# First image's statistics by channel and half with long rows for the matrices, and layer 1's transfers by four columns

## The chip, the cores and the metric

The kernel runs on one core of one Trainium2 chip. The metric is the device time of one execution in microseconds (us), the median over several runs. Everything is in float32.

## What is computed

The input x has 4 images of 64 channels and 256 x 256 pixels. Two layers follow each other, each with a group norm over pairs of channels in front and a residual sum behind:

```python
def _gn(v, G=32, eps=1e-5):
    g = v.reshape(B_, G, C_ // G, H_, W_)
    m = jnp.mean(g, axis=(2, 3, 4), keepdims=True)
    s = jnp.var(g, axis=(2, 3, 4), keepdims=True)
    return ((g - m) / jnp.sqrt(s + eps)).reshape(v.shape)

x = x + _L0_conv_ref(_gn(x), L0_conv_w1, L0_conv_w_dw, L0_conv_w_out, L0_conv_ln_w, L0_conv_ln_b)
x = x + _L1_conv_ref(_gn(x), L1_conv_w_ih, L1_conv_w_hh, L1_conv_b_ih, L1_conv_b_hh)
```

Layer 0 takes 64 channels to 384 by a 1x1 convolution, applies a 3x3 depthwise convolution, splits into q, k and v, multiplies the Fourier transforms of q and k in patches of 8 x 8 pixels (a circular convolution), applies a layer norm over the channels, multiplies by v and projects back to 64 channels. Layer 1 is a gated recurrent unit that runs over the columns of the image, one after the other. The state of a column's pixel is its new value; its input are the three neighbours in the column before:

```python
def step(prev_col, cur_col):
    nb = jnp.concatenate([pad, prev_col, pad], axis=1)
    x = jnp.concatenate([nb[:, :-2], nb[:, 1:-1], nb[:, 2:]], axis=-1)
    new = _gru_cell(x.reshape(B * H, 3 * Cf), cur_col.reshape(B * H, Cf), w_ih, w_hh, b_ih, b_hh).reshape(B, H, Cf)
    return (new, new)
```

## The kernel before

The host hands over x with columns ahead of rows, and besides that xh, a copy cut into windows of 10 x 10 pixels (100 values, HALO) for every 8 x 8 patch. All instructions of an engine run in the order in which the program names them (the class InOrder); a DMA is issued by an engine's queue in that same order, so a DMA that waits holds up everything that the program puts after it on that queue. The queues used are SP's (most transfers), POOL's (xq, seen, the writing of the matrices) and ACT's (weights).

**Preamble.** Three things are prepared. First, the depthwise taps and the Fourier matrices are merged into matrices of 100 x 64 per channel: 32 rounds of small matmuls into PSUM (psb), each copied by ACT into the tile ts, 96 KB per partition. Three DMAs on POOL's queue write ts to the DRAM tile t_all (3 x 3200 KB), laid out [3, 8, 100, 1024], so that one fetch of 16 channels' matrices later reads one contiguous block of 400 KB (100 rows of 4 KB). Second, the statistics of the first image: it is read in 8 steps of 2 MB (xc), each by two DMAs of 64 partitions, one for the left half of the image and one for the right (function piece, lines 206 to 210), and VectorE takes bn_stats of 512 elements. norm_of_pieces (line 84) then averages over the pairs of channels and the halves with a 128 x 128 matrix (avg2) and leaves scale and shift in sc0. Third, the weights: hh, w1, g, wo, ln and taps on ACT's queue at the start, wi, wh and bias on the same queue after the statistics, in thirteen DMAs.

**Layer 0** runs in 32 blocks (n), eight for each image. The pools for its tiles (big, xp, tp, wk) are opened after the preamble's are closed, in the same memory. A block's input xq comes in four quarters (load, line 296, on POOL's queue; normalize, line 303, on ACT or VectorE, with small memsets on POOL at the image's edges). Then:

- pointwise, 3 x 16 units: the 1x1 convolution, evicted to the tile h;
- circular, twice: transform multiplies h with matrices t, which fetch (line 329) brings four ahead from t_all on SP's queue; products q * k on VectorE in buffers of the pool wk (seven of 4 KB per partition, lines 289 and 290); inverse back to the pixels in z;
- values: v from h with the last eight matrices;
- layer_norm in slices between the other work, with its statistics in the tile lnst;
- finish(n - 1), which lies in the next block: residual loads xr (x of the block, SP's queue), gate transposes and multiplies, project adds to xr, and store writes it to the DRAM tile x1 (two DMAs of 64 partitions for each of four units u; the last unit's store is put off to the circular stage).

Beside this the next image's statistics are taken: look loads a piece of 4 columns (two DMAs of 64 partitions on POOL's queue) into a wk buffer, count takes bn_stats of it, four times per block (24 of the 32 blocks).

**Layer 1** runs over 256 columns w. x1 is [4, 64, 256, 256], columns ahead of rows. Two images stand side by side on the 128 partitions, channels of one on 0 to 63 and of the other on 64 to 127, with the pairs of images arranged differently in even and odd columns (SLOTS), so that each of TensorE's four 64 x 64 quarters has work. A pair of columns is loaded by three DMAs (load_columns, one of 128 partitions for the even column, two of 64 for the odd one), in rows of 1 KB; stored likewise by three (in add, line 767, after POOL's sum with the raw values); and two more DMAs copy the normalized columns to the other half of the partitions (xt, in normalize, line 748). Columns are loaded 16 ahead and normalized 8 ahead, in tiles of eight columns (WB). column(w) issues the matmuls of the gates r, n and z in two parts of the column; state(w, part) applies sigmoid, tanh and the update on ACT and VectorE.

Of the kernel before, what the change touches and what calls it, by code (L numbers as in the profile page):

```python
# [83 lines left out]
def norm_of_pieces(nc, st, t, psum, eps, sc):  # L84

    m_all, d, total, mean = t[:, 128:136], t[:, 136:144], t[:, 144:145], t[:, 145:146]
    nc.vector.tensor_copy(m_all, st[:, :, 0])
    nc.vector.tensor_reduce(total, m_all, mybir.AxisListType.X, ALU.add)  # L90
    yield
    pm = psum()
    nc.tensor.matmul(pm, lhsT=t[:, 0:P], rhs=total, start=True, stop=True)
    nc.vector.tensor_copy(mean, pm)
    nc.vector.tensor_tensor(d, m_all, mean.to_broadcast([P, 8]), ALU.subtract)
    nc.vector.tensor_tensor(d, d, d, ALU.mult)
    nc.vector.tensor_tensor(d, d, st[:, :, 1], ALU.add)
    nc.vector.tensor_reduce(total, d, mybir.AxisListType.X, ALU.add)
    yield
    pv = psum()  # L100
    nc.tensor.matmul(pv, lhsT=t[:, 0:P], rhs=total, start=True, stop=True)
    nc.scalar.activation(sc[:, 1:2], pv, AF.Sqrt, bias=eps, scale=1.0)
    nc.vector.reciprocal(sc[:, 1:2], sc[:, 1:2])
    nc.vector.scalar_tensor_tensor(sc[:, 0:1], mean, -1.0, sc[:, 1:2], ALU.mult, ALU.mult)
    yield
# [57 lines left out]
def tile_conv_then_gru(  # L163
# [14 lines left out]
    avg2: bass.AP,  # L178
    out: bass.AP,
# [5 lines left out]
    x1 = dram.tile([B, C, W, H], F32, tag="x1", name="x1")  # L185


    t_all = dram.tile([3, 8, HALO, 16 * NS], F32, tag="t_all", name="t_all")


    ident = const.tile([P, P], F32, tag="ident", name="ident")
    make_identity(tc.nc, ident)
    hh_sb = const.tile([P, P], F32, tag="hh", name="hh_sb")
    nc.scalar.dma_start(hh_sb, hh)
    eps = const.tile([P, 1], F32, tag="eps", name="eps")
    nc.gpsimd.memset(eps, EPS)
    w1_sb = const.tile([P, HID], F32, tag="w1", name="w1_sb")
    nc.scalar.dma_start(w1_sb, w1.rearrange("a c o -> (a c) o"))
    g_sb = const.tile([P, 2, 2, NS], F32, tag="g", name="g_sb")
    nc.scalar.dma_start(g_sb, g12.rearrange("a s r n p -> (a s) r n p"))  # L200
    wo_sb = const.tile([P, 2, C], F32, tag="wo", name="wo_sb")
    nc.scalar.dma_start(wo_sb, w_out.rearrange("a f t c -> (a f) t c"))
    ln_sb = const.tile([P, 2, 2], F32, tag="ln", name="ln_sb")
    nc.scalar.dma_start(ln_sb, ln.rearrange("a f n t -> (a f) n t"))

    def piece(of, b, i, w, n):

        for half in range(2):
            w0 = half * (W // 2) + i * (W // 16) + w
            yield slice(half * C, (half + 1) * C), of[b, :, w0 : w0 + n, :].rearrange("c w h -> c (w h)")  # L210
# [6 lines left out]
    with tc.tile_pool(name="xa", bufs=3) as xa, tc.tile_pool(name="sta", bufs=1) as sta, tc.tile_pool(  # L217
# [4 lines left out]
        for i in range(4):  # L222
            nc.scalar.dma_start(bt[32 * i : 32 * i + 9], taps[i])
            nc.sync.dma_start(wd[32 * i : 32 * i + 9], w_dw)
        avg4 = sta.tile([P, 1024], F32, tag="avg4", name="avg4_0")
        nc.sync.dma_start(avg4[:, 0:P], avg2)
        ts = sta.tile([HALO, 3 * P, NS], F32, tag="ts", name="ts")
        banks = bps.tile([P, 8, 512], F32, tag="b", name="psb")
        for i in range(32):
# [14 lines left out]
        for i in range(3):  # L244
            nc.gpsimd.dma_start(
                t_all[i].rearrange("n p k -> p n k"),
                ts[:, i * P : (i + 1) * P].rearrange("p (n c) k -> p n (c k)", n=8),
            )
        for i in range(8):
            xc = xa.tile([P, 4096], F32, tag="xc", name=f"xc_{i}")  # L250
            for at, of in piece(x, 0, i, 0, 16):
                nc.sync.dma_start(xc[at], of)
            for k in range(8):
                nc.vector.bn_stats(bn0[:, k, :], xc[:, 512 * k : 512 * k + 512])
            nc.vector.bn_aggr(st0[:, i, :], bn0)
        for _ in norm_of_pieces(nc, st0, avg4, lambda: banks[:, 0, 0:1], eps, sc0[:, 0]):
            pass
    wi = const.tile([P, 9, C], F32, tag="wi", name="wi")
    wh = const.tile([P, 3, C], F32, tag="wh", name="wh")
    for a in range(2):  # L260
        at = slice(a * C, (a + 1) * C)
        for g in range(3):
            nc.scalar.dma_start(wi[at, 3 * g : 3 * g + 3, :], w_ih[g].rearrange("t c o -> c t o"))
            nc.scalar.dma_start(wh[at, g, :], w_hh[g])
    bias_sb = const.tile([P, 6], F32, tag="bias", name="bias_sb")
    nc.scalar.dma_start(bias_sb, bias.rearrange("a o n -> (a o) n"))
# [5 lines left out]

    st1 = const.tile([P, NBLK, 2], F32, tag="st1", name="st1")
    with ExitStack() as s:
        big = s.enter_context(tc.tile_pool(name="big", bufs=1))
        xp = s.enter_context(tc.tile_pool(name="xp", bufs=4))
# [18 lines left out]
        xq = {}  # L295

        def load(n, jq):

            t = xp.tile([P, 16, HALO], F32, tag="xq", name=f"xq_{n}_{jq}")
            nc.gpsimd.dma_start(t, xh[n, :, 16 * jq : 16 * jq + 16, :])  # L300
            xq[n, jq] = t

# [26 lines left out]
        def fetch(count):  # L329
            while len(streamed) < min(count, NBLK * 24):  # L330
                m, r = divmod(len(streamed), 24)
                t = tp.tile([P, 16, NS], F32, tag="t", name=f"t_{m}_{r}")
                nc.sync.dma_start(t[0:HALO].rearrange("p c k -> p (c k)"), t_all[order[r][0], order[r][1]])
# [124 lines left out]
        def layer_norm(n):  # L458

            st = big.tile([P, 2, NP // 2, 6], F32, tag="lnst", name=f"lnst_{n}")  # L460
# [128 lines left out]
        def store(n, u, xr):  # L589
            b, r0, c0 = n // 8, (n % 8) * 32 + (u // 2) * 8, (u % 2) * P  # L590
            for g in range(2):
                nc.sync.dma_start(
                    x1[b, :, r0 + 16 * g : r0 + 16 * g + 8, c0 : c0 + P],
                    xr[g * C : (g + 1) * C],
                )

        def look(n, k, t):

            for at, of in piece(x, n // 8 + 1, n % 8, 4 * k, 4):
                nc.gpsimd.dma_start(t[at], of)  # L600

        def count(n, k, t):
            for i in range(2):
                nc.vector.bn_stats(bn0[:, 2 * k + i, :], t[:, 512 * i : 512 * i + 512])
            if k == 3:
                nc.vector.bn_aggr(st0[:, n % 8, :], bn0)
# [12 lines left out]
        for jq in range(4):  # L619
            load(0, jq)  # L620
        for jq in range(4):
            normalize(0, jq)
        norm = None
        for n in range(NBLK + 1):
# [4 lines left out]
            if n == NBLK:  # L629
                for _ in norm:  # L630
                    pass
            if n:
# [5 lines left out]
            more = n // 8 + 1 < B  # L638
            if more:
                seen = work(f"seen0_{n}")  # L640
                look(n, 0, seen)
            circular(n, 0, lambda sp: count(n, 0, seen) if more and sp == 1 else None)
            if more:
                seen = work(f"seen1_{n}")
                look(n, 1, seen)
            for unit in range(16):
                pointwise(n, 1, unit, unit in (5, 8, 11, 14))
                if more and unit in (8, 14):
                    count(n, unit // 7, seen)
                    look(n, unit // 7 + 1, seen)  # L650
# [3 lines left out]
            def beside(sp):  # L654
                next(norm)
                if more and sp == 1:
                    count(n, 3, seen)
# [3 lines left out]
            if more and n % 8 == 7:  # L661
                t = work(f"avg4_{n}")
                nc.gpsimd.dma_start(t[:, 0:P], avg2)
                image = norm_of_pieces(nc, st0, t, lambda: psum()[:, 0, 0:1], eps, sc0[:, n // 8 + 1])
# [53 lines left out]
    with ExitStack() as s:  # L718
        rawp = s.enter_context(tc.tile_pool(name="raw", bufs=3))
# [5 lines left out]
        def columns(m, w):  # L725

            yield m[:, :, w, :].rearrange("(k a) c h -> (a c) k h", k=NPAIR), slice(0, P), 0
            for half in range(2):
                b0 = SLOTS[1][0][half]
                yield m[b0 : b0 + 2, :, w + 1, :].rearrange("b c h -> c b h"), slice(half * C, half * C + C), 1  # L730

        def load_columns(w):
            n, i = w // WB, w % WB
            if i == 0:
                raws[n] = rawp.tile([P, 2, WB, H], F32, tag="raw", name=f"raw_{n}")
            for of, at, j in columns(x1, w):
                nc.sync.dma_start(raws[n][at, :, i + j], of)
# [10 lines left out]
        def normalize(w, slot):  # L748
            n, i = w // WB, w % WB
            if i == slot == 0:  # L750
                new_columns(n)
            nc.scalar.activation(
                xns[n][:, slot, i],
                raws[n][:, slot, i],
# [4 lines left out]
            if slot and i % 2:  # L759

                for half in range(2):
                    nc.sync.dma_start(
                        xts[n][half * C : (half + 1) * C, i - 1 : i + 1],
                        xns[n][(1 - half) * C : (2 - half) * C, half, i - 1 : i + 1],
                    )

        def add(w):
            n, i = w // WB, w % WB
            nc.gpsimd.tensor_tensor(
                raws[n][:, :, i], raws[n][:, :, i], stcols[n][:, :, i, 1 : H + 1], ALU.add  # L770
            )
            if i % 2:
                for of, at, j in columns(out, w - 1):
                    nc.sync.dma_start(of, raws[n][at, :, i - 1 + j])
# [152 lines left out]
```

## Time and profile before

| | us |
|---|---|
| median of 3 runs | 5883.06 |
| lowest and highest run | 5861.34, 5891.94 |
| the profiled execution | 5869.95 |
| its span in the trace | 5868.2 |
| preamble, up to the first matmul of layer 0 | 138.3 |
| layer 0, up to layer 1's first loads | 4338.1 |
| layer 1, first matmul with xt | 4357.8 |
| TensorE's granted clock, mean | 0.994 |

Of the page's six parts the first two (busy time of each engine, and the span in forty slices of 147 us) tell which engine is full in which stage. Parts 3 and 6 hold the transfers: SP's queue carried 520152 packets and 633.59 MB (40.0% of the sixteen DMA engines' time), POOL's 37776 packets and 165.24 MB (9.5%), and the instruction queue 996 packets and 16.32 MB. All compute instructions have one line number, that of the class InOrder, so groups go by the names of tiles: psring is the PSUM ring of layer 0, pshr, psni, pshz and pshn are the gates' banks in layer 1, raw and xn the columns as loaded and normalized.

### The profile page before, as it was taken

How to read it: one execution, taken by the hardware profiler on the slowest of the kernel's cores; microseconds unless marked ns; L12 is line 12 of the kernel's file. 1: busy time of each engine (PE TensorE's matmuls, PEld its weight loads, DVE VectorE, ACT ScalarE, POOL GpSimd, SP SyncE). 2: the span in 40 equal slices, each digit the busy share in tenths (PEclk: the TensorE clock that was granted, in tenths of full speed). 3: DMA queues.
4: the chain of work that ended last, by engine and by line, in shares of the span. 5: the costliest groups of instructions: out<-in, count | busy, mean ns of one | idle time of the engine just before them, and what ended most of it. 6: DMA issues, size and time to landing. Idle time of an engine off the chain costs nothing. (4 is left out here: it accounts for less than half of the span.)

```text
span 5868.2 us, 278629 instructions
## 1 busy us (share of the span) xinstructions
PE 5479.9 (93%) x127196; PEld 4762.6 (81%) x127196; DVE 4080.5 (70%) x9593; ACT 3475.4 (59%) x4604; POOL 500.8 (9%) x797
## 2 busy tenths in 40 slices
PE   2999999999999999999999999999979999999998
PEld 1878888888788878887888888878868888888888
DVE  2776777777767777777677767766667777776766
ACT  2556566665565656655655666556556666666655
POOL 0000000000000000000000000000002122222222
PEclk9999999999999999999999999999989999999999
DMA  8455555555555555555555454544444444444443
GB/s 225 135 156 147 151 151 155 154 142 152 157 147 154 150 151 159 141 150 159 150 152 150 140 143 126 142 139 125 137 114 116 116 116 117 115 117 113 116 114 81
DMA packets 561916, 818.04 MB, mean 139 GB/s; under 512 B 41353, under 2 KB 435373, under 8 KB 559677
## 3 DMA queue, kind: packets, MB, share of 16 engines
q1 hardware_dynamic: 520152, 633.59, 40.0%
q0 software_dynamic: 37776, 165.24, 9.5%
q8 instruction: 996, 16.32, 1.2%
q10 hardware_dynamic: 2808, 1.38, 0.1%
q14 instruction: 184, 1.50, 0.1%
HBM read 622.46 MB, written 144.05 MB: 131 GB/s over the span
## 5 line engine op out<-in xcount | busy, mean ns | idle before, releaser
L157 PEld LDWEIGHTS psring<-h,t 100*32 100x32 f32 x40960 | 1334.1, 115 | 294.0 <-issue 175.2
L157 PE MATMUL psring<-h,t 100*32 100x128 f32 x40960 | 1445.2, 274 | 105.9 <-issue 37.7
L157 PE MATMUL psring<-w_sb,xq 64*100 64x128 f32 x24576 | 1403.2, 271 | 55.7 <-POOL xq L157 40.2
L157 PEld LDWEIGHTS psring<-w_sb,xq 64*100 64x100 f32 x24576 | 1357.6, 164 | 117.0 <-issue 50.2
L157 ACT COPY h<-psring 100x1024 f32<-100x1024 f32 x1274 | 1205.5, 1027 | 161.4 <-PE psring L157 155.2
L157 DVE TENSOR_TENSOR pr<-psring,q 128x512 f32<-128x512 f32 (+1 forms) x576 | 463.3, 857 | 308.8 <-PE psring L157 234.8
L157 DVE BATCH_NORM_STATS2 lnst<-z 128x6 f32<-128x64 f32 x4096 | 545.4, 214 | 117.6 <-ACT z L157 117.6
L157 DVE TENSOR_TENSOR z<-z,lnm 128x1024 f32<-128x1024 f32 x512 | 612.7, 1218 | 8.8
L157 ACT COPY q<-psring 128x1024 f32<-128x1024 f32 x256 | 259.3, 1013 | 596.8 <-PE psring L157 358.9
L157 ACT ACTIVATE z<-pshz,b_rz 128x288 f32<-128x288 f32 (+7 forms) x510 | 242.6, 476 | 519.8 <-PE pshz L157 519.7
L157 PE MATMUL pshr<-st,wi 64*64 64x144 f32 (+7 forms) x12240 | 510.5, 270 | 34.9 <-issue 20.9
L157 PE MATMUL psni<-st,wi 64*64 64x144 f32 (+7 forms) x12240 | 510.4, 270 | 24.4 <-issue 22.4
L157 PE MATMUL pshz<-st,wi 64*64 64x144 f32 (+7 forms) x12240 | 510.8, 270 | 23.1 <-issue 21.9
L157 ACT COPY z<-psring 128x2048 f32<-128x2048 f32 x128 | 238.9, 1867 | 446.7 <-PE psring L157 441.7
L157 PE MATMUL psring<-pr,g_sb 32*64 32x512 f32 x8192 | 494.8, 594 | 5.7 <-issue 5.5
L157 ACT ACTIVATE y<-psring,ln_sb 128x512 f32<-128x512 f32 x512 | 372.5, 781 | 200.5 <-PE psring L157 197.0
L157 PEld LDWEIGHTS psni<-st,wi 64*64 64x64 f32 x12240 | 446.5, 133 | 45.5 <-issue 34.4
L157 PEld LDWEIGHTS pshr<-st,wi 64*64 64x64 f32 x12240 | 422.3, 133 | 52.3 <-issue 49.5
L157 DVE COPY h<-psring 100x1024 f32<-100x1024 f32 x262 | 320.3, 1223 | 198.7 <-PE psring L157 194.7
L157 PEld LDWEIGHTS pshz<-st,wi 64*64 64x64 f32 x12240 | 424.9, 133 | 37.3 <-issue 36.4
L157 DVE SCALAR_TENSOR_TENSOR g<-z,xn 128x288 f32<-128x288 f32 (+7 forms) x510 | 218.4, 428 | 311.9 <-ACT z L157 310.0
L157 POOL TENSOR_TENSOR raw<-raw,st 128x512 f32<-128x512 f32 x256 | 303.7, 1186 | 1146.0 <-ACT xn L157 548.1
(98 smaller groups left out, 7377.9 us busy)
## 6 DMA issues: line engine op xcount, KB each, us to landing
t<-t_all SPq DMA_DIRECT2D x768, 400.0 KB
xq<-in_xh POOLq DMA_DIRECT2D x128, 800.0 KB, 4.6
xr<-in_x SPq DMA_DIRECT2D x256, 256.0 KB
x<-xr SPq DMA_DIRECT2D x256, 256.0 KB
seen<-in_x POOLq DMA_DIRECT2D x192, 256.0 KB, 4.1
raw<-x SPq DMA_DIRECT2D x128, 256.0 KB
raw<-x SPq DMA_DIRECT2D x256, 128.0 KB
xt<-xn SPq DMA_DIRECT2D x256, 128.0 KB
```

The lines of the kernel that those rows point to most:

```text
L157: return self.tc.keep_in_program_order(got(*args, **kwargs))
```

## The change

**Preamble.** x is read by (channel, half of the image) on all 128 partitions, in 16 steps of 1 MB with one DMA each and five buffers. norm_of_pieces gets two matrices (sums): one averages in the order of these partitions, the other carries the mean over to the order of the normalization. The DRAM tile t_all becomes [3, 100, 8, 1024]: ts is written in rows of 32 KB, and a fetch reads 100 rows of 4 KB at a pitch of 32 KB. The first two of the three writes are named before the third kind is computed. The pool xp is opened ahead of the preamble's pools, and the first block's four loads of xq come right after the writes on POOL's queue. The weights move to SP's queue, between the sixth and seventh piece of x, in one DMA each.

**Layer 0.** store writes even and odd columns to separate halves of x1, in four DMAs per unit instead of two. Pieces of the next image are loaded on 128 partitions; those of two columns go into lnst, which becomes one tile for the whole layer, and two of four columns go into one wk buffer.

**Layer 1.** x1 and the output are [2, 4, 64, 128, 256], even and odd columns apart (the host puts them together again). Four columns are loaded by three DMAs in rows of 2 KB, stored by three, and copied to xt by two, spread over four steps of w. Tiles of raw columns hold four columns, in seven buffers. Before the first step four columns are normalized instead of nine; the function ahead then catches up to eight.

```diff
-    x1 = dram.tile([B, C, W, H], F32, tag="x1", name="x1")
-    t_all = dram.tile([3, 8, HALO, 16 * NS], F32, tag="t_all", name="t_all")
+    x1 = dram.tile([2, B, C, W // 2, H], F32, tag="x1", name="x1")
+    t_all = dram.tile([3, HALO, 8, 16 * NS], F32, tag="t_all", name="t_all")
+    layer0 = ExitStack()
+    xp = layer0.enter_context(tc.tile_pool(name="xp", bufs=4))
...
     def piece(of, b, i, w, n):
-        for half in range(2):
-            w0 = half * (W // 2) + i * (W // 16) + w
-            yield slice(half * C, (half + 1) * C), of[b, :, w0 : w0 + n, :].rearrange("c w h -> c (w h)")
+        w0 = i * (W // 16) + w
+        return of[b].rearrange("c (a w) h -> (c a) w h", a=2)[:, w0 : w0 + n, :].rearrange("p w h -> p (w h)")
...
+        def keep_matrices(i):
+            nc.gpsimd.dma_start(
+                t_all[i].rearrange("p n k -> p (n k)"),
+                ts[:, i * P : (i + 1) * P].rearrange("p c k -> p (c k)"),
+            )
...
-        for i in range(3):
-            nc.gpsimd.dma_start(
-                t_all[i].rearrange("n p k -> p n k"),
-                ts[:, i * P : (i + 1) * P].rearrange("p (n c) k -> p n (c k)", n=8),
-            )
-        for i in range(8):
-            xc = xa.tile([P, 4096], F32, tag="xc", name=f"xc_{i}")
-            for at, of in piece(x, 0, i, 0, 16):
-                nc.sync.dma_start(xc[at], of)
+            if i == 15:
+                keep_matrices(0)
+                keep_matrices(1)
+        keep_matrices(2)
+        for jq in range(4):
+            load(0, jq)
+        def seen_piece(i):
+            xc = xa.tile([P, 2048], F32, tag="xc", name=f"xc_{i}")
+            nc.sync.dma_start(xc, piece(x, 0, i // 2, i % 2 * 8, 8))
+            for k in range(4):
+                nc.vector.bn_stats(bn0[:, i % 2 * 4 + k, :], xc[:, 512 * k : 512 * k + 512])
+            if i % 2:
+                nc.vector.bn_aggr(st0[:, i // 2, :], bn0)
...
     pm = psum()
-    nc.tensor.matmul(pm, lhsT=t[:, 0:P], rhs=total, start=True, stop=True)
+    for i in range(2):
+        nc.tensor.matmul(pm[:, i : i + 1], lhsT=t[:, P * i : P * i + P], rhs=total, start=True, stop=True)
...
             for g in range(2):
-                nc.sync.dma_start(
-                    x1[b, :, r0 + 16 * g : r0 + 16 * g + 8, c0 : c0 + P],
-                    xr[g * C : (g + 1) * C],
-                )
+                at = r0 // 2 + 8 * g
+                for odd in range(2):
+                    nc.sync.dma_start(x1[odd, b, :, at : at + 4, c0 : c0 + P], xr[g * C : (g + 1) * C, odd::2])
...
+            def beside_first(sp):
+                if more and sp in (0, 3):
+                    count(n, 2 * (sp // 3), seen)
+                    look(n, 2 * (sp // 3) + 2, seen)
+
+            circular(n, 0, beside_first)
             if more:
-                seen = work(f"seen1_{n}")
-                look(n, 1, seen)
+                four = work(f"seen_{n}")
+                look(n, 8, four)
...
-            if slot and i % 2:
+            if slot and i % 4 == 3:
                 for half in range(2):
                     nc.sync.dma_start(
-                        xts[n][half * C : (half + 1) * C, i - 1 : i + 1],
-                        xns[n][(1 - half) * C : (2 - half) * C, half, i - 1 : i + 1],
+                        xts[n][half * C : (half + 1) * C, i - 3 : i + 1],
+                        xns[n][(1 - half) * C : (2 - half) * C, half, i - 3 : i + 1],
                     )
...
+        def ahead(w):
+            return min(2 * w + 4, w + WB + 1, W)
...
             add(w)
-            if i % 2 and w + 2 * WB < W:
-                load_columns(w + 2 * WB - 1)
+            if i >= 2:
+                store_columns(w - i, i - 2)
+            elif i == 0 and w:
+                store_columns(w - 4, 2)
+            if i < 3 and w - i + 2 * WB < W:
+                load_columns(w - i + 2 * WB, i)
+        store_columns(W - 4, 2)
```

## The prediction

> **What bounds the kernel now.** I read the page first (busy shares and the forty slices), then a table of busy time by stretches of the span, then the waits of TensorE in each stage, then the timeline where the stretches show TensorE idle. From the page:
>
> ```profile
> PE 5479.9 (93%) x127196; PEld 4762.6 (81%) x127196; DVE 4080.5 (70%) x9593; ACT 3475.4 (59%) x4604; POOL 500.8 (9%) x797
> ...
> PE   2999999999999999999999999999979999999998
> ...
> DMA  8455555555555555555555454544444444444443
> ```
>
> TensorE is full in every slice but two: the first (147 us, two tenths) and the one where layer 0 hands over to layer 1 (seven tenths). Of 5868.2 us it is idle 388 us. The stretches say where:
>
> ```profile
> 20.00:40.00 20.00, 15.35 (x106) 6.36 (x108) 10.43 (x18) 11.56 (x12) 0.00 (x0) 1.00 1.01 216
> ...
> 60.00:80.00 20.00, 0.00 (x0) 0.00 (x0) 10.43 (x18) 0.00 (x0) 0.00 (x0) 1.00 1.01 250
> 80.00:100.00 20.00, 1.00 (x4) 0.95 (x4) 11.59 (x25) 0.00 (x0) 0.00 (x0) 1.00 0.98 285
> 100.00:120.00 20.00, 0.14 (x1) 0.05 (x1) 0.32 (x2) 1.55 (x2) 0.00 (x0) 1.00 0.73 225
> ```
>
> (Columns: PE, PEld, DVE, ACT, POOL busy; granted clock; DMA share; GB/s.) The preamble is bound by the DMA engines: they are full, yet move only 216 GB/s while the first image is read alone. Then a second hold, after that read is over:
>
> ```profile
> 97.95 0.56 PE L157 MATMUL psb<-avg 128*128 128x1 f32 x2 [42.60 <-issue]
> ...
> 126.77 52.92 SPq L157 DMA_DIRECT2D t<-t_all  x11
> ...
> 127.57 2.17 POOL L157 DMA_DIRECT2D xq<-in_xh  x4 [70.28 <-DMA t<-t_all]
> ...
> 138.31 6.25 PE L157 MATMUL psring<-w_sb,xq 64*100 64x128 f32 x64 [38.17 <-POOL xq L157]
> ```
>
> The statistics are done at 102 us, but layer 0's first tiles of input (xq) are requested only at 127.6 us, when the matrices have landed in t_all, and the first matmul of layer 0 waits until 138.3. So 36 us lie between statistics and work.
>
> Layer 0 (180 to 4280 us) has TensorE busy 3970 of 4100 us; a block takes (4284.1 - 245.2) / 31 = 130.3 us, and all named waits of TensorE there add to 127 us, 46 of them with no releaser, 36 on ACT's last copy of h, 15 on the matrices. Nothing in it is bound by a transfer for long. Layer 1, in a part without its ends (4400 to 5700 us), first stretches and then waits:
>
> ```profile
> 4400.00:5700.00 1300.00, 1211.14 (x40650) 1153.83 (x40646) 918.50 (x2209) 792.25 (x1768) 267.04 (x277) 1.00 0.42 116
> 5700.00:5765.00 65.00, 59.25 (x1984) 56.15 (x1980) 44.39 (x108) 38.37 (x86) 13.13 (x13) 1.00 0.42 115
> 5765.00:5810.00 45.00, 42.78 (x1432) 40.29 (x1428) 32.59 (x79) 28.05 (x63) 8.57 (x9) 1.00 0.32 83
> 5810.00:5850.00 40.00, 39.66 (x1369) 38.70 (x1365) 30.40 (x74) 19.77 (x46) 9.51 (x8) 1.00 0.21 57
> ```
>
> ```profile
> PE pshz L157 <- issue: 26.0, 47, 1.2
> PE pshr L157 <- issue: 25.6, 53, 1.2
> PE psni L157 <- issue: 19.5, 27, 1.7
> PE pshr L157 <- DVE st L157: 13.4, 7, 1.9
> ```
>
> TensorE waits for no transfer here. Its gaps are "issue": 71 us in 1300, in 127 pieces, and in the timeline they stand at multiples of about 4 us. A column is 184 matmuls and as many weight loads in 5.88 us, some 63 instructions per us, so 256 of them last 4.1 us. As the loads run out (share 0.42, 0.32, 0.21) the rate rises from 31.3 to 31.8 and 34.2 matmuls per us.
>
> [...] the two half-image pieces of 2 MB come every 10.1 us, 207 GB/s, with the engines' share at 1, while the 128-partition xq loads run at 312 to 315 GB/s. [...]
>
> **The change, part by part.**
>
> *1. Preamble.* Removed: the half-partition reads, twelve weight DMAs on ACT's queue (100 to 127 us, ACT can't normalize behind them), and the wait of xq for the memory that the matrices' buffer gives back, since xq's pool is now allocated ahead of it. Added: one 128x128x1 matmul (0.3 us), nine constant loads among the image's pieces on SP. What must move before the first matmul: image 16.8 MB, matrices 9.8 (issued at 44 and 56 us as before, paced by ACT's copies), constants and taps 1.5, first xq 0.8: 28.9 MB. The rate is unknown for this mix; nearest rows: 312 to 331 GB/s (xq alone; 85 to 95 us), 250 (60 to 80 us, held by the half-partition stream). I take 300: 96 us from 2.5, then 2 us to land, 1.7 normalize, 0.4 memset: about 103 us instead of 138.3. DVE isn't the bound (16 pieces x 2.6 us = 42 us). At 330 GB/s the first matmul is at 94, at 250 at 122. If [...]the image still takes 10 us per 2 MB, the matrices still land near 125 and only the ACT and memory wait goes: 8 us. Gain: 35 us, bounds 8 to 45. xq follows the matrices in the same POOL queue, so its pieces arrive at the same spacing as now and the ramp from 138 to 149 us moves along unchanged. The first t loads (4 of 400 KB) have 22 us of pointwise units ahead of their use.
>
> *2. Matrices read with 32 KB pitch.* Still 100 rows of 4 KB per fetch. Taken at nothing; the cover is the four-deep fetch, TensorE waits 15 us for it over 32 blocks. In the chain of waits a fetch takes 3.4 to 8.4 us from issue to landing; if its usual 5 us grew to 7, the circular stages, which use a matrix every 2.7 us with four in flight, would still just fit.
>
> *3. Stores to x1 by odd and even.* Four DMAs per unit instead of two, 256 more on SP at 0.64 us (two x<-xr take 1.28): +1.3 us per unit, four units a block. Behind a store on SP stand the next residual load, which has 4 us to spare before its add, and the t fetches for the start of the circular stage, issued at 2115.4 directly behind such a store and used at 2122. Late by 1.3 us they land about when needed. I take +0.4 us a block, 13 us; bounds 0 and 48 (1.5 us a block in full).
>
> *4. Statistics of later images.* Eight POOL DMAs a block become six of 128 partitions, and all but two of them use the layer norm's own buffer, so one working buffer fewer is held in the first circular stage. There DVE waited for a store to give a buffer back (2.46 us at 2120). TensorE felt little of it (0.2 us there), so -0.4 us a block in 24 blocks, -10 us; bounds -25 and +10. The same eight bn_stats a block stay. Parts 2 to 4 sum to about 0.
>
> *5. Entry of layer 1.* 24 loads on SP took 15.05 us, and xt stood behind them until 4353.3, landing at 4357.7. Now 12 loads (7.6 us) and four columns to normalize first (8 x 0.54 us) instead of nine: xt issued near 4348, but behind the same 4 MB in the queue (14 us at 300 GB/s). Gain 3 us, bounds 0 to 6. The doubled normalization in columns 1 to 5 takes ACT from 3.6 to 4.8 us of 5.9: covered.
>
> *6. Layer 1's stream.* Eight DMAs on SP per four columns instead of sixteen, rows of 2 KB (xt 4 KB) for 1 KB. No transfer is waited for now, so fewer issues gain nothing themselves: SP spends 792 us waiting in this layer. xt is asked for five columns ahead, not seven, 29 us against 4.4 to land. What can change is the block fetch of TensorE's instructions. From 1 KB packets (17 GB/s per engine: 116 / 0.42 / 16) and 6.4 KB ones (20 GB/s) I estimate a share of 0.38. Between the rows for 0.42 and 0.32 (31.3 and 31.8 matmuls per us, 1.7%, 25 us over the layer) that is 10 us; bursts spread over all columns may give more. I take 12 us; bounds +20 (longer rows hold the fetch up longer) and -60 (half of the way to 34.2).
>
> Sum: 35 + 0 + 3 + 12 = 50 us, so 5868.2 becomes 5818. The profiled execution took 5869.95, 13 us under the median of 5883.06; the same 50 us from the median, rounded, give 5832.
>
> **Rivals.**
> (a) The DMA engines don't speed up: x at 207 GB/s as before, part 1 gives 8 us and parts 5 and 6 15: about 5860 from the median, within 0.5%. For: share 1.0 says full engines. Against: xq's 312 GB/s at the same share.
> (b) Instruction fetch is freed: with half the packets the layer-1 rate goes half of the way to the tail's 34.2, 60 us instead of 12: 5784. For: gaps vanish with the load. Against: the tail also has ACT free of normalization.
> (c) Slower: the t fetches come late. From a landing of more than about 10 us (four in flight, one used per 2.7 us), by pitch or by SP's stores ahead, TensorE waits at every fetch of the 16 in circular stages. At 0.4 us each, 6.4 us x 32 = 205 us, less 50: about 6038. It decides above some 80 us, 2.5 us a block. For: fetches already appear on TensorE's wait list. Against: 4 KB rows at 256 KB pitch (seen) land in 4.1 us.
> (d) SP's extra stores cost the full 48 us: 5867, no measurable change.
>
> **How the numbers follow.** A measurement of this kernel tells 0.5%, 29 us, from no change: bounds 5854 and 5912. Chances: forecast (5800 to 5854) 0.52, (b) 0.17, (a) and (d) together 0.19, (c) 0.12. So faster 0.69, same 0.19, slower 0.12. The range from 5765 to 5895 leaves out (c) and the far end of (b). The likeliest case's own range is 5800 to 5854.
>
> **What would show it.** Right: image pieces of 2 MB every 6 to 7 us, GB/s near 300 in the first 100 us, xq issued near 57 us, first layer-0 matmul at 94 to 122, xt landed near 4320 or before (4357.7 less the shift); "issue" in layer 1 at 55 to 70 us; block period 130.3 within 0.5. Wrong: a block period of 131 or more with "DMA t" among TensorE's waits, a first matmul after 125, or "issue" in layer 1 above 90 us.

## The result and the profile after

The changed kernel takes 5878.22 us (median of 12 runs, 5859.22 to 5896.2), the kernel before, run beside it, 5885.4 (12 runs, 5861.34 to 5896.7). The ratio is 0.9993, 95% interval 0.9977 to 1.0009: no change that this measurement can tell. 5832 had been forecast, and the range ended at 5895.

The profiled execution has a span of 5885.9 us, 17.7 more than the one of before; single executions of either kernel differ by up to 37 us, so the traces are used for where time went, and the ratios for how much. From the page:

```profile
PE 5466.0 (93%) x127204; PEld 4757.4 (81%) x127204; DVE 4078.9 (69%) x9593; ACT 3472.2 (59%) x4604; POOL 476.1 (8%) x749
...
PE   4999999999999999999999999999979888899888
...
DMA  7555555555555555555555455454443434434332
```

TensorE does the same work. Its first slice is fuller (4 tenths, 2 before), and in six of the last nine slices an 8 stands where a 9 was: time was won at the start and lost in layer 1.

**Preamble.** The stretches (columns as before the change: PE, PEld, DVE, ACT, POOL busy; clock; DMA share; GB/s), then the timeline:

```profile
20.00:40.00 20.00, 18.07 (x142) 7.80 (x145) 13.26 (x23) 15.96 (x17) 0.43 (x1) 1.00 0.92 354
...
60.00:80.00 20.00, 0.00 (x0) 0.00 (x0) 4.78 (x9) 0.00 (x0) 0.00 (x0) 1.00 0.95 349
80.00:100.00 20.00, 0.00 (x0) 0.00 (x0) 8.23 (x14) 0.00 (x0) 0.00 (x0) 1.00 0.59 242
```

```profile
51.83 2.13 POOL L158 DMA_DIRECT2D xq<-in_xh  x4
62.56 2.47 DVE L158 BATCH_NORM_STATS2 bn<-xc 128x6 f32<-128x512 f32 x4 [11.22 <-DMA xc<-in_x]
...
97.62 2.48 DVE L158 BATCH_NORM_STATS2 bn<-xc 128x6 f32<-128x512 f32 x4 [1.91 <-DMA xc<-in_x]
...
107.99 16.88 PE L158 MATMUL psring<-w_sb,xq 64*100 64x128 f32 x256 [4.30 <-POOL xq L158]
```

From 20 to 40 us, with the image and a few weights on the way, 354 GB/s move (216 before), and the DMA engines' share is 0.92 (1.01 before). The first matmul of layer 0 starts at 108.0 us instead of 138.3. What ends the preamble has changed: the matrices (from 39.6 us on) and xq (from 51.8) share the engines with the rest of the image, VectorE waits 11 us for a piece, and the last piece comes at 97.6. The statistics are done at 105.6 us, later than before (102.0), but xq has landed by then and nothing stands behind them any more.

**Layer 0 and entry of layer 1.** One activation per block, in the layer norm, serves as a clock (duration; first and last start):

```profile
L157 ACT ACTIVATE lnm<-psring,eps x32: 377/378/383, 245.2 to 4284.1; 128x128 f32<-128x128 f32 x32
```

is the kernel before, and the changed one has

```profile
L158 ACT ACTIVATE lnm<-psring,eps x32: 377/378/383, 209.2 to 4258.7; 128x128 f32<-128x128 f32 x32
```

A block takes (4258.7 - 209.2) / 31 = 130.63 us, 130.29 before. Two waits of TensorE there, from 150 to 4280 us (total, times, longest):

```profile
PE psring L158 <- issue: 39.7, 52, 2.5
PE psring L158 <- DMA t<-t_all: 36.4, 54, 1.3
```

Before, the wait for the matrices was 13.7 us, 31 times, in the same stretch.

**Layer 1**, waits of TensorE in 1300 us without its ends (4370 to 5670 us):

```profile
PE pshz L158 <- issue: 44.8, 39, 2.1
PE pshr L158 <- issue: 43.3, 44, 2.0
PE psni L158 <- issue: 21.8, 21, 2.0
...
PE pshn L158 <- issue: 7.1, 8, 1.5
```

That is 117 us in 112 gaps of 1.04 us, where it was 71 us in 128 gaps of 0.56 us. There are no more gaps than before; each is nearly twice as long. The layer lasts 1545.2 us from the first to the last matmul of gate r with xt, 1496.1 before:

```profile
L157 PE MATMUL pshr<-xt,wh x2040: 253/269/500, 4357.8 to 5853.9; 64*64 64x140 f32 x7, 64*64 64x118 f32 x7, 64*64 64x121 f32 x7, 64*64 64x132 f32 x7
```

```profile
L158 PE MATMUL pshr<-xt,wh x2040: 254/269/499, 4328.4 to 5873.6; 64*64 64x140 f32 x7, 64*64 64x118 f32 x7, 64*64 64x121 f32 x7, 64*64 64x132 f32 x7
```

The two traces add up as follows: preamble and ramp (to the first lnm) -36.0, layer 0 +10.6, entry of layer 1 -4.0, layer 1 +49.1, tail -2.0: +17.7 us. They are two single executions; how well such a difference repeats, experiments 1 and 2 show.

### The profile page after: what moved, and what is told of

The parts are those of the page before. It is cut to its first block, busy times and chain, and to the rows that moved or that the text cites. A ratio compares the mean times of both kernels' runs of the same rounds, so it can differ in the third digit from the quotient of the medians.

```text
span 5885.9 us, 278118 instructions
## 1 busy us (share of the span) xinstructions
PE 5466.0 (93%) x127204; PEld 4757.4 (81%) x127204; DVE 4078.9 (69%) x9593; ACT 3472.2 (59%) x4604; POOL 476.1 (8%) x749
## 4 chain that ended last, share of the span: by engine, by line
PE 71%; issue 4%; DMA 4%; ACT 3%; DVE 1%; SPq 1%; POOLq 0%; ACTq 0%; DVEq 0%
PE psring L158 48%; PE pshz L158 8%; PE pshr L158 8%; PE psni L158 6%; DMA t<-t_all 4%; PE pshn L158 2%; ACT v L158 1%; ACT z L158 1%; SPq L158 1%; ACT h L158 0%; DVE z L158 0%; DVE lnst L158 0%; DVE xr L158 0%; ACT xq L158 0%; DMA xt<-xn 0%
## 5 line engine op out<-in xcount | busy, mean ns | idle before, releaser
L158 PEld LDWEIGHTS pshr<-st,wi 64*64 64x64 f32 x12240 | 425.7, 133 | 58.1 <-issue 55.2
L158 DVE TENSOR_TENSOR y<-psring,y 128x1024 f32<-128x1024 f32 x256 | 312.4, 1221 | 127.2 <-ACT y L158 121.9
```

The lines of the kernel that those rows point to most:

```text
L158: return self.tc.keep_in_program_order(got(*args, **kwargs))
```

## The experiments

The theory after the result (A): the preamble's gain is real, and layer 1 loses it because rows of 2 KB hold up the block fetch of TensorE's instructions. Rivals: the loss is in layer 0 (B), in the order of issue of layer 1 (C), or in the size of its transfers, not of the rows (D). Below, "issue" is always the sum of these waits of TensorE over 1300 us inside layer 1, starting 42 us after its first matmul with xt. Ratios are to the kernel before, run on the same chip; chips differ (its median was 5885 us at first, 5909 to 5917 in what follows).

**1. The preamble alone.** Layer 1's code, store and the layouts of x1 and the output as before:

```diff
-    x1 = dram.tile([2, B, C, W // 2, H], F32, tag="x1", name="x1")
+    x1 = dram.tile([B, C, W, H], F32, tag="x1", name="x1")
...
-            of, to = columns(x1, w, i)
-            nc.sync.dma_start(to.rearrange("p k w h -> p k (w h)"), of)
+            for of, at, j in columns(x1, w):
+                nc.sync.dma_start(raws[n][at, :, i + j], of)
```

> The changed kernel with layer 1, the stores to x1 and the layouts of x1 and the output put back as before; the preamble, the statistics and the long rows for the matrices stay. Theory A (the preamble's 36 us are real and are lost again in layer 1, where longer rows hold up the fetch of TensorE's instruction blocks): first matmul of layer 0 near 108 us, 'issue' waits of TensorE in layer 1 back at about 70 to 80 us per 1300 us, median 30 to 36 us under before, ratio 0.994 to 0.995. Theory B (the loss is in layer 0, by the matrices' pitch of 32 KB): block period stays at 130.6 us and the ratio near 0.996 to 0.998.

Measured: 5873.73 against 5908.96 us, ratio 0.9937 (0.992 to 0.9954). The preamble is worth what was forecast of it. "Issue" was 96.4 us in 156 gaps of 0.62: more than in the first trace of before (71.3 us) with the same code, so one trace's sum of "issue" is good to some 25 us; the mean length of a gap repeats better (0.56 there). Layer 1 took 1529.5 us, which is 33 more than in that trace:

```profile
L158 PE MATMUL pshr<-xt,wh x2040: 254/269/499, 4333.5 to 5863.0; 64*64 64x140 f32 x7, 64*64 64x118 f32 x7, 64*64 64x121 f32 x7, 64*64 64x132 f32 x7
```

So most of the 49 us above may be a difference between executions or chips. The block period, 130.61, was the one that theory B named, though the ratio was not.

**2. Layer 1 alone**, the reverse: the kernel before with layer 1, store and layouts of the change.

> The kernel before with only layer 1 by four columns, the layouts of x1 and the output, and the stores split by odd and even. Theory A: first matmul of layer 0 at 138 us as before, 'issue' in layer 1 at 110 to 130 us per 1300 us, median 25 to 40 us above before, ratio 1.004 to 1.007. If instead the loss comes from layer 0's matrices: ratio 0.998 to 1.001. If the split stores cost layer 0 its 10 us: block period 130.6 us here and 130.3 in the run with the preamble only.

Measured: 5941.79 us, ratio 1.0054 (1.0036 to 1.0071); "issue" 110.7 us in 107 gaps of 1.03. The change is two halves that cancel: 0.9937 x 1.0054 = 0.9991, and 0.9993 was measured for both. Against experiment 1, on the same chip, layer 1 is only 9.8 us longer (1539.3 us):

```profile
L157 PE MATMUL pshr<-xt,wh x2040: 253/269/499, 4385.9 to 5925.2; 64*64 64x140 f32 x7, 64*64 64x118 f32 x7, 64*64 64x121 f32 x7, 64*64 64x132 f32 x7
```

The block period is 131.01 us, 130.61 in experiment 1, and that makes 12 us over layer 0 (the granted clock of these executions, 0.990 and 0.993, could make as much, if the time went with it: 0.3% of layer 0). So the 0.54% may be a cost of both layers, as the last case of the expectation had it, and layer 1's own share is known only as between 10 and 49 us.

**3. Rows or transfers?** Two kernels with the changed preamble and the changed order of layer 1, every load and store in two DMAs, one for each pair of images k. One has rows of 2 KB:

```diff
-            nc.sync.dma_start(to.rearrange("p k w h -> p k (w h)"), of)
+            for k in range(NPAIR):
+                nc.sync.dma_start(to.rearrange("p k w h -> p k (w h)")[:, k], of[:, k])
```

The other the same, but x1 and the output laid out as before, so that the two columns of a transfer are apart (w : w + 3 : 2) and the rows have 1 KB; its stores to x1 in layer 0 are two DMAs per unit, as before.

> The changed kernel, four columns at a time, but with x1 and the output in their old layouts (rows of 1 KB) and every load and store of layer 1 issued as two DMAs, one for each pair of images; xt stays at 4 KB. Theory A (length of rows): 'issue' in layer 1 near 70 to 80 us per 1300 us with gaps of 0.6 us on average, ratio 0.994 to 0.996 to before. Rival C (not the rows: the order of issue, SP held by POOL's sums and then letting go of several transfers at once): 'issue' at 110 us or more, gaps of 1 us, as in the changed kernel, ratio 0.999 to 1.002.

> The changed kernel with every load and store of layer 1 issued as two DMAs, one for each pair of images; rows of 2 KB as changed. Same count, order and size of transfers as the run with rows of 1 KB; only the rows differ (and the stores of layer 0, in four DMAs per unit here, two there). Theory A: 'issue' at 110 us or more per 1300 us, gaps of 1 us, ratio 0.999 to 1.001. Rival C: the same as the run with rows of 1 KB. Rival D (size of a transfer, not of a row): smaller transfers help here too, 'issue' under 90 us.

Measured: rows of 1 KB 5833.64 us, ratio 0.9866 (0.9848 to 0.9884), "issue" 67.7 in 101 gaps of 0.67; rows of 2 KB 5817.85 us, ratio 0.9849 (0.9831 to 0.9868), "issue" 55.6 in 96 gaps of 0.58. The waits of the latter (4383 to 5683 us), to be held against the changed kernel's above:

```profile
PE pshr L158 <- issue: 24.1, 38, 1.5
PE pshz L158 <- issue: 19.3, 34, 1.3
...
PE psni L158 <- issue: 9.2, 18, 1.2
```

Theory A falls: at the same size of transfers, rows of 2 KB have no longer gaps than rows of 1 KB, and the intervals of the two ratios overlap. C falls too: order and rows are those of the changed kernel, and cutting the transfers alone takes "issue" from 117 to 56 us and layer 1 from 1545 to 1475.5 us (from 1539.3 against experiment 2, on the same chip and at the same granted clock of 0.990, so the clock isn't the cause). D holds. One thing goes along with the size: cut in two, the same bytes are also issued over more time (0.6 us for an issue), and no run here tells this spreading from the size itself.

**4. Cut into four**: each load and store of the changed kernel by k and by column, rows of 1 KB.

```diff
-            nc.sync.dma_start(to.rearrange("p k w h -> p k (w h)"), of)
+            for k in range(NPAIR):
+                for j in range(2):
+                    nc.sync.dma_start(to[:, k, j], of[:, k, j * H : (j + 1) * H])
```

> The changed kernel with every load and store of layer 1 cut into four DMAs (one for each pair of images and each column, rows of 1 KB[...]). Theory D[...]: gaps shorter than the 0.6 us of the runs cut in two, 0.3 to 0.4 us on average, 'issue' under 45 us per 1300 us, ratio to before 0.981 to 0.984. Rival E (cutting helps only until other costs take over: 24 issues of 0.4 to 0.6 us per four columns on SP, more completions): 'issue' at 55 to 70 us, ratio 0.984 to 0.988.

Measured: 5848.63 us, ratio 0.9877 (0.9856 to 0.9899), "issue" 55.2 in 116 gaps of 0.48. Rival E's numbers: no gain over two parts, and theory D missed its own. Gaps of 0.48 us are shorter than with two parts, but not 0.3 to 0.4; xt, with 256 KB per DMA, was not cut here, which may be why. Of the 20 us between the traces of this run and of the one with rows of 2 KB in two parts, 13 lie in the entry of layer 1 (82.5 us from the last lnm to the first matmul with xt, 69.5 there), where twice as many loads are issued ahead of xt.

**5. Pairs of columns, cut in two**: experiment 1 with its layer 1 by pairs, each DMA cut by k.

```diff
-                nc.sync.dma_start(raws[n][at, :, i + j], of)
+                for k in range(NPAIR):
+                    nc.sync.dma_start(raws[n][at, k, i + j], of[:, k])
```

> The kernel with the preamble only (layer 1 by pairs of columns, as before), with every load and store of layer 1 cut into two DMAs, one for each pair of images[...]. Theory D: 'issue' falls from 96 to 50 to 65 us per 1300 us, ratio to before 0.984 to 0.988 (0.994 uncut). Rival F (order of issue counts in the old order too, all of a pair's transfers come in one bunch): 'issue' stays at 85 us or more, ratio 0.992 to 0.995.

Measured: 5827.25 us, ratio 0.9839 (0.9817 to 0.986); from 4381 to 5681 us:

```profile
PE pshr L158 <- issue: 18.5, 48, 0.8
PE pshz L158 <- issue: 18.3, 45, 0.9
PE psni L158 <- issue: 8.3, 23, 0.8
```

46.5 us in 121 gaps of 0.38: a little under what theory D had said, and the longest gap is 0.9 us (1.5 uncut). So the old order gains by the cut as well. It pays 11 us for it at the entry of layer 1 (81.9 us, 70.9 in experiment 1).

**6. Layer 0 too**: experiment 3 with rows of 2 KB, and the fetches of matrices (t) and the loads of xq in two DMAs each.

```diff
-                nc.sync.dma_start(t[0:HALO].rearrange("p c k -> p (c k)"), t_all[order[r][0], :, order[r][1]])
+                for g in range(2):
+                    nc.sync.dma_start(
+                        t[0:HALO, 8 * g : 8 * g + 8].rearrange("p c k -> p (c k)"),
+                        t_all[order[r][0], :, order[r][1], 8 * NS * g : 8 * NS * g + 8 * NS],
+                    )
```

> The changed kernel with layer 1's loads and stores cut in two (as in the run with rows of 2 KB), and in layer 0 the fetches of matrices (t) and the loads of xq cut in two as well. Theory D: layer 0's 'issue' waits of about 40 us and part of the short stops of the weight loads shrink, block period 129.8 to 130.3 us instead of 130.9, ratio 0.980 to 0.983. Rival: layer 0's TensorE issues fewer instructions per us and its fetches are rarely late, or 24 more issues on SP per block delay the fetches of t: period 130.8 or more, ratio 0.985 or above.

Measured: 5778.92 us, ratio 0.9764 (0.9746 to 0.9781), block period 128.77 us (130.86 in experiment 3). Layer 0 gains by cuts as well; experiment 9 shows where. Here a cut shortens the rows too (t from 4 to 2 KB, xq from 6.4 to 3.2), so in layer 0 size and rows are not told apart.

**7. The stores left out**, uncut transfers:

```diff
         def store_columns(w, i):
+            if 16 <= w < W - 16:
+                return
```

> The changed kernel with the stores of the output left out for columns 16 to 239, so a third of layer 1's bytes is not moved and the output is not the reference's there. If the 'issue' gaps come from data transfers in front of the instruction fetch: 'issue' falls from 117 to under 70 us per 1300 us and layer 1 shortens by 40 us or more. If they are TensorE's own (fixed per block of 256 instructions): unchanged near 110 us.

Measured (one execution): span 5815.5 us, layer 1 1475.2 us; from 4370 to 5670 us:

```profile
PE pshr L158 <- issue: 30.0, 29, 2.0
PE pshz L158 <- issue: 19.9, 20, 2.0
PE pshn L158 <- issue: 10.3, 9, 2.0
PE psni L158 <- issue: 8.4, 11, 1.7
```

68.6 us in 69 gaps of 0.99. With fewer transfers of the same size the gaps are fewer, not shorter; with smaller ones they are shorter. So they depend on the data transfers and are not a fixed cost of TensorE.

**8. All cuts, layer 1 by pairs**: experiment 5 with the cuts of experiment 6 in layer 0.

> The preamble of the change, layer 1 by pairs of columns as before with every load and store cut in two by pair of images, stores to x1 in two DMAs per unit as before, and in layer 0 the fetches of t and the loads of xq cut in two. If the costs add: layer 1 as in the run with pairs cut in two (1478 us from first to last xt matmul), layer 0's block period 128.5 to 129.0 us, ratio 0.972 to 0.977; under the run with four columns and the same cuts in layer 0 (0.9764) by 0 to 20 us, which would be what layer 0 pays for stores split by odd and even.

Measured: 5772.57 us, ratio 0.9749 (0.9729 to 0.977), block period 128.73, layer 1 1465.9 us. The gains add. Against experiment 6 the intervals overlap, so by time stores split by odd and even weren't told apart from stores in two DMAs.

**9. Only the matrices' fetches cut** in layer 0, xq whole; layer 1 as in experiment 6.

> The changed kernel with layer 1's loads and stores cut in two, and in layer 0 only the fetches of t cut in two (200 KB each), the loads of xq whole. If it is t's fetches (two smaller ones land sooner, 'DMA t' leaves TensorE's waits[...]): nearly all of the 40 us between the runs without (0.9849) and with both cuts (0.9764), ratio 0.976 to 0.979. If it is xq's loads[...]: ratio 0.983 to 0.986.

Measured: 5773.26 us, ratio 0.975 (0.9731 to 0.9768), at or a little below the window. It is t. From 180 to 4200 us, after cutting t:

```profile
PE psring L158 <- issue: 38.7, 45, 2.3
...
PE psring L158 <- DMA t<-t_all: 2.8, 5, 1.0
```

The wait for matrices is nearly gone (30.2 us in the same stretch of experiment 3), "issue" falls by 9 us (from 47.4). So most of what is named here is the wait for t, and less of it the gaps of the fetch of instructions.

**10. t and xq in four**, otherwise experiment 8:

```diff
-                for g in range(2):
+                for g in range(4):
                     nc.sync.dma_start(
-                        t[0:HALO, 8 * g : 8 * g + 8].rearrange("p c k -> p (c k)"),
-                        t_all[order[r][0], :, order[r][1], 8 * NS * g : 8 * NS * g + 8 * NS],
+                        t[0:HALO, 4 * g : 4 * g + 4].rearrange("p c k -> p (c k)"),
+                        t_all[order[r][0], :, order[r][1], 4 * NS * g : 4 * NS * (g + 1)],
                     )
```

> As the run with all cuts and layer 1 by pairs, but t and xq cut in four (t 100 KB, xq 200 KB). [...] block period 128.0 to 128.5, ratio 0.969 to 0.973. If issue and completion of 96 fetches a block on SP take over: period 129 or more, ratio 0.975 to 0.980.

Measured: 5728.63 us, ratio 0.9678 (0.9658 to 0.9697), below the first window (0.969), though its interval reaches into it; block period 127.72 us. Layer 0's waits, 180 to 4160 us:

```profile
PE psring L158 <- issue: 14.2, 18, 1.6
...
PE psring L158 <- DMA t<-t_all: 10.9, 14, 1.4
```

This is the best version, 3.2% under the kernel before.

**11. The remaining transfers cut too**: residual loads, stores to x1 and xt in two.

```diff
-                        xts[n][half * C : (half + 1) * C, i - 1 : i + 1],
-                        xns[n][(1 - half) * C : (2 - half) * C, half, i - 1 : i + 1],
+                    for j in range(i - 1, i + 1):
+                        nc.sync.dma_start(
+                            xts[n][half * C : (half + 1) * C, j], xns[n][(1 - half) * C : (2 - half) * C, half, j]
```

> As the run with t and xq in four, with the residual loads, the stores to x1 and the copies to xt cut in two as well[...]. [...] 'issue' in layer 1 under 40 us per 1300 us, ratio 0.963 to 0.967. If SP's own time takes over (16 more issues per block and 4 more per pair of columns at 0.5 us, with t's fetches behind them): ratio 0.968 to 0.975.

Measured: 5817.92 us, ratio 0.9828 (0.9813 to 0.9843), worse than either line. "Issue" in layer 1 fell to 31.8 us, under the 40 of the first line, but SP's queue has next to no pause left. From 4400 to 5600 us its DMA instructions add to 1097 us of 1200, in experiment 10 to 988, in the kernel before to 528:

```profile
4799.53 4.23 SPq L158 DMA_DIRECT2D out<-raw  x6
4803.81 4.54 SPq L158 DMA_DIRECT2D raw<-x  x6
4808.45 2.99 SPq L158 DMA_DIRECT2D xt<-xn  x4
4811.53 4.79 SPq L158 DMA_DIRECT2D out<-raw  x6
```

Sixteen issues take 12.0 us in these lines, and two columns took 11.5 us in experiment 10 (1467.9 us for 255 columns). ACT now waits for raw, which it didn't there, and TensorE for ACT (4328 to 5628 us):

```profile
PE pshz L158 <- ACT z L158: 46.7, 34, 3.0
...
ACT xn L158 <- DMA raw<-x: 152.9, 60, 4.9
```

In layer 0 the wait for t came back (31.7 us), its fetches standing behind more issues. Layer 1 took 1520.0 us. So the cut has an end: the issuing queue's time.

The layer-1 runs by size of the largest load or store:

| kernel | KB | "issue", us | gaps | mean, us |
|---|---|---|---|---|
| changed | 512 | 117.0 | 112 | 1.04 |
| layer 1 alone | 512 | 110.7 | 107 | 1.03 |
| changed, no stores | 512 | 68.6 | 69 | 0.99 |
| before | 256 | 71.3 | 128 | 0.56 |
| preamble alone | 256 | 96.4 | 156 | 0.62 |
| four columns in two, 1 KB rows | 256 | 67.7 | 101 | 0.67 |
| four columns in two, 2 KB rows | 256 | 55.6 | 96 | 0.58 |
| four columns in four | 128 | 55.2 | 116 | 0.48 |
| pairs in two | 128 | 46.5 | 121 | 0.38 |
| four columns in two, 2 KB rows (6) | 256 | 68.5 | 119 | 0.58 |
| the same (9) | 256 | 61.5 | 116 | 0.53 |
| pairs in two (8) | 128 | 40.3 | 105 | 0.38 |
| pairs in two (10) | 128 | 43.2 | 111 | 0.39 |
| pairs in two, xt too (11) | 128 | 31.8 | 78 | 0.41 |

In the last five rows the number of the experiment stands in brackets.

That the gaps are waits for instructions can be read from the kept traces, which have every packet of the instruction queue with its start and length. In the 1300 us of each run, take all gaps above 0.15 us in which TensorE neither multiplies nor loads weights. From one gap to the next there are, in eight or nine cases of ten, a whole multiple of 256 instructions (to within 16). In every run but experiment 11, where TensorE waits for ACT too, 93 to 100% of the gaps end 1.1 to 1.8 us after the end of such a packet (median 1.4); by chance it would be 17%, as a packet comes every 4.1 us. The packet itself takes 1.1 to 1.2 us on average in every kernel, with no longer time where the gaps are longer (1.11 in the changed kernel, 1.16 in experiment 8). So what grows with the size of the data transfers is the time before the fetch starts. Estimated from the grid of the gaps, 95% of the fetches start within 3.0 us of a block's first instruction in the changed kernel, 2.7 in the one before, 2.6 and 2.7 in experiment 3, 2.2 in experiment 5 and 2.0 in experiment 8.

## Why the prediction was wrong

By the parts of the prediction:

*Part 1, preamble, 35 us forecast.* Right in size, in part by luck: 36.0 us in the traces, 0.63% or 37 us by experiment 1. The rate rose as it had been read from the trace of before: 354 GB/s from 20 to 40 us, 216 before, though the reads of 128 partitions also come in shorter packets (8 KB, 16 before), and no run tells the two apart. But the first matmul came 30.3 us earlier, not 35, and the other 5.7 us came in the ramp behind it, which the text had said would move along unchanged. Two terms were off and cancelled: the rate was above the 300 taken (31.4 MB moved in the first 100 us), and the last to arrive is the image's tail, not xq, since the matrices and all of xq took part of the engines from it.

*Parts 2 to 4: matrices at a 32 KB pitch, taken at nothing; split stores, 13 us lost; statistics, 10 us won.* Together about 0 was forecast, +10.6 us came in the traces. The wait for t rose from 14 to 36 us, as the text had feared of stores ahead of the fetches. The other traces with t uncut point to the stores. From 180 to 4160 us, TensorE waits 12 to 19 us for t in the four with two stores per unit (before, experiments 1 and 5, and 3 with rows of 1 KB), and 26 to 35 us in the five with four (the changed kernel, experiments 2, 4 and 7, and 3 with rows of 2 KB). Experiment 2, with 26 us, has the matrices without the pitch; experiment 1, with 17, has them with it. What this is worth in time is not settled: the block periods of the two groups overlap (130.28 to 130.67 us, and 130.61 to 131.01).

*Part 5, entry of layer 1, 3 us.* 4.0 in the traces.

*Part 6, layer 1's stream, 12 us to be won.* **This step failed, in sign.** It took the DMA share as what makes the instruction fetch late, read a rate between the rows for shares 0.42 and 0.32, and bounded the loss at 20 us. The share did fall, about as estimated (0.40 in the stretch above, 0.38 estimated), and the gaps doubled in length all the same; in experiments 5 and 8 the share rises to 0.44 and 0.45 and the gaps shrink. What decides is the size of a single transfer (with the spreading named in experiment 3): the change doubled the loads and stores from 256 to 512 KB, and the text counted this only as fewer issues. It named a block's fetch held up, but by longer rows; experiment 3 shows rows have no part in it. The term taken at -12 measures +49 us in the first pair of traces and +10 us between experiments 1 and 2. Layer 1 with its stores costs 0.54% (0.36 to 0.71), some 32 us, by experiment 2, of which layer 0 may have 12.

Of the text's own signs, first matmul at 108.0 us and block period within 0.5 us stood for right, and "issue" at 117 us, above 90, for wrong. That last sign alone was weak: experiment 1 has 96.4 us with layer 1's old code. That the time lies within the outer range of 5765 to 5895 owes nothing to the reasoning: the forecast gain and a loss that had not been forecast cancelled.

Three small slips in its figures change nothing: 50 us from 5883.06 is 5833, not 5832; the waits of 127 and 15 us in layer 0 belong to the stretch up to 4320 us, not 4280 (119 and 13.7 there); half of the way to 34.2 matmuls per us is about 66 us, not 60.

Rivals (a) and (d) gave about the right time for wrong reasons: (a) had the DMA engines no faster in the preamble, (d) had all of the loss in layer 0's stores. Rival (c), late fetches of t, was in the right place with a tenth of its size (23 us more of waiting, where it had 205). None of the rivals had a loss by size of transfers.

The grid fits the packets of the instruction queue: in the kernel before, 127196 matmuls and as many weight loads on 996 packets of 16 KB are 255 to a packet, and the 317 packets in its 1300 us come every 4.1 us. A fifth to a half of that number show as a gap (69 to 156 in the table), of 0.4 to 1.0 us on average. Why a large transfer makes the fetch start late stays open: no trace or run here shows what the fetch waits behind.

## What to carry to other kernels

Where TensorE runs many short instructions, look for "issue" gaps on the grid of 256 instructions, and read their mean length against the size of the transfers in flight: here they were a price of large DMAs, and the list of waits gives them no releaser. Cutting the transfers in two or four, with bytes and order unchanged, was worth more here than the whole change (3.2% for experiment 10 over before, about 0.6% of it the new preamble), up to the point where the issuing queue is full (1097 of 1200 us in experiment 11). Loads that a stage waits for at its start were better left whole here: cutting them from 24 DMAs to 48 cost 11 us at the entry of layer 1. And a saving in the number of DMAs gained nothing here, as that queue still waited: before the change SP spent 792 us of layer 1 waiting.

## What the runs showed of the hardware that was not expected

- The gap of TensorE's issue follows the size of a single transfer: 0.99 to 1.04 us with 512 KB, 0.53 to 0.67 with 256 KB, 0.38 to 0.48 with 128 KB; rows of 1 or 2 KB give 0.67 and 0.58. The gaps end 1.4 us (median) after a packet of the instruction queue, and that packet takes 1.1 to 1.2 us whatever the size of the data transfers.
- Cutting the 400 KB fetches of 100 rows in two removed TensorE's wait for them (30.2 to 2.8 us) and shortened the block period from 130.86 to 128.92 us, 60 us over the layer. The waits listed for TensorE explain 34 of these (131.7 to 97.7 us). Nearly all of the rest is shorter busy time of TensorE for the same matmuls (3912.8 to 3889.2 us from the first lnm to the last). It goes with the cut and not with the granted clock: 3906 to 3913 us in the nine traces with t uncut (the kernel before, at a clock of 0.994, has 3910.8), 3889 to 3890 us in the three with t in two (0.994 to 0.995); on one chip, experiments 4, 5 and 7 have 3907 to 3910, experiment 6 has 3890. Why it is shorter is open.
- DMA issues from SP cost 0.6 to 0.7 us each in layer 1. At 14 per pair of columns they were hidden (layer 1 1467.9 us, experiment 10), at 16 they were not (1520.0 us, experiment 11).
